# New place tables for a planned convolution and attention kernel, and another split of additions and products between VectorE and GpSimd

## The chip, the cores and the metric

The kernel runs on one core of a Trainium2 chip. Its time is the device time of one execution in microseconds (us). Five engines work beside each other, each through its own list of instructions in a fixed order: TensorE (PE; its weight loads are shown as PEld), VectorE (DVE), ScalarE (ACT), GpSimd (POOL) and SyncE (SP), which starts the DMAs. An instruction that waits holds up everything behind it on its engine.

## The reference

The input is x of shape 16 x 256 x 56 x 56 in float32. Two layers follow each other, each with a residual:

```python
x = x + _L0_conv_ref(_gn(x), ...)   # layer 0
x = x + _L1_conv_ref(_gn(x), ...)   # layer 1

# layer 0: sign of the input, then three dilated 3x3 convolutions (4 groups of
# 64 channels), each with binary weights, PReLU, shifts; summed; a norm over channels
for i, d in enumerate((1, 3, 5)):
    y = conv(sign(x + bias), bin_weight(w[i]), dilation=d, groups=4) + cb[i] - move1[i]
    y = where(y >= 0, y, alpha[i] * y) + move2[i]
    out = out + y
out = layer_norm_over_channels(out) * gamma + beta

# layer 1: 8 heads, 3x3 neighbourhood attention, 64 inner channels
q, k, v = qkv_w @ x + qkv_b
k = unfold(k) + dc_b + dwconv(k) + rpb       # 9 neighbours
v = unfold(v) + dc_b + dwconv(v)
attn = softmax((q * k).sum(channel), over the 9 neighbours)
out = proj_w @ (attn * v).sum(neighbours) + proj_b
```

`_gn` is a group norm with 32 groups.

## The kernel before

The 16 images are worked one after the other, each in two units (u = 0 and 1) of 128 partitions x 784 elements per channel group. An image goes through these stages, and each stage's operations are numbered from 0 in the order in which the program names them:

- `stats`, `norm0`, `sign`: ACT sums x and its squares (L570) and writes the signs (L594) into one set of tiles, `sgn`, that the convolutions of the image read.
- `conv0`, `conv1` (function `conv`): for each of 4 channel groups and 3 dilations, 36 matmuls on PE (L644), then ACT and DVE work on the PSUM banks (L663, L673, L678, L683). The third dilation's part is kept in a tile `rl` and added to `ct` at L689, an operation that goes through `either`.
- `var`, `root`, `mean`, `scale` (function `channel_norm`): the norm over channels; DVE subtracts the mean (L755) and scales (L765); the residual is added at L778, through `either`; ACT squares the sum (L782).
- `fold`: the second group norm is folded into the attention weights (L803 on POOL, L825 on PE). `qkv0`, `qkv1`: PE (L862), ACT writes q, k and v (L880).
- `prod0`, `prod1`: nine products of q with a shifted k for each unit (L915, through `either`). `term0`, `term1`: PE sums them over channels (L937).
- `soft0`, `soft1`: DVE transposes (L950, L972), maximum (L961), subtraction (L962), sum and reciprocal; ACT the exponential (L966); the product with the reciprocal goes through `either` (L971).
- `value0`, `value1` (function `attend`): for each neighbour PE spreads the weights (L986), DVE multiplies by v (L997), and a sum is kept in a tile `m`: the eight additions go through `either` (L1010); the tenth term is added by DVE (L1015).
- `proj0`, `proj1`: PE (L1027), and DVE adds the residual (L1037); then the store.

`either` emits an operation for GpSimd, or for VectorE where the operation's number stands in the table `ON_VECTOR` of its stage. A number of an operation that does not go through `either` has no effect; `soft0: (3,)` is of that kind, since operation 3 of `soft` is the subtraction that is always VectorE's.

No engine's order is written out. A class `Plan` collects all operations with what they read and write. Each has a place: `PERIOD` times its image's number, plus its entry in the table `ORDER`. A stage's name ends in `^` for the first image and in `$` for the last, and has no mark for the 14 images between. `Plan.emit` sorts by place and again and again takes the first operation whose inputs have been emitted and for which tiles are free; that gives every engine its order. A very low place therefore means "as soon as inputs and tiles allow". Tiles are few: four pairs of PSUM banks, five tiles `p`, three `m`, three `xt`, one set each of q, k and v.

Of the kernel before, what the change touches and what calls it, by code (L numbers as in the profile page):

```python
# [70 lines left out]
class Op:  # L71
    def __init__(self, place, emit, bufs):
# [6 lines left out]
PERIOD = 126.77  # L79
ORDER = {  # L80
    "first^": (-497.79,),
    "weights^": (
        -540.59, -276.27, -472.85, -121.02, 1.79, -121.01, -33.38, -40.08, -310.38, -8.87, -87.51, 10.76,
        -121.02, -347.57, 1.55, 12.14, -692.71, -322.65, -525.75, -97.97, -407.33, -195.77, -129.92,
        -262.19, -190.53, 10.75, -82.95, 37.61, -222.6, -117.13, -281.25, -133.31, 10.59, -72.96, 32.23,
        19.36, 12.13, -419.49, -79.69, -153.17, -260.86, -336.22,
    ),
    "second^": (
        61.97, 77.89, 59.61, -394.88, -231.37, -525.72, -317.93, 89.98, -351.54, -320.24, -170.43, -99.11,
    ),  # L90
    "start^": (
        -37.89, -330.85, 1.52, -87.54, -489.3, -643.61, -435.35, -192.82, -270.37, -108.68, -149.06,
        -278.79, -2012.74, -534.49, -502.69, -254.52, -75.19, 2.17, -46.62, -149.05, -203.19, -76.32,
        -254.55, -263.41, -527.85, -211.59, -216.21, -271.53, -72.59, -316.59, -388.45, -417.16, -608.13,
        -117.13, -276.59, 2.55, -250.76, -130.26, -368.41, -212.02, 3.89, -950.45, -407.55, -2282.23,
        -22.71, -513.74, -817.71, -764.21, -253.24, -287.46, -359.77, -118.23, -713.07, 35.52, 34.89,
        -41.66, -43.35, -258.45, -522.62, -624.21, -243.88, -289.86, -487.62, -51.52, -254.56, -583.14,
        -559.88, -516.73, -568.78, -425.01, -172.57, -282.11, -200.04,
    ),
    "conv0^": (  # L100
        -138.79, -276.48, -171.15, 36.21, -36.36, -506.31, -29.89, -243.93, 49.82, -784.24, -355.82,
        -293.64, -34.24, -130.27, -258.79, -37.09, 33.51, -139.51, -301.96, 37.42, 27.55, 69.97, 39.93,
        -631.57, -218.19, 72.59, 57.81, -355.85, -543.32, -414.61, 63.22, -365.99, 68.63, -658.09, 72.02,
        -37.08, -292.03, -552.29, -122.08, -314.82, -533.21, -570.33, -391.64, -204.63, -28.82, -120.38,
        -389.94, -254.56, -94.86, -138.42, -3.94, 38.26,
    ),
    "load0^": (65.19,),
    "var0^": (65.64, 75.51, -158.49, 8.33, -251.92, 76.54, -575.76, 19.98),
    "root0^": (-131.94, -804.87, -238.36, -98.85, -212.3, -189.81, -984.51, -512.94, -159.93, -30.98),
    "mean0^": (-97.24, -331.38, -195.77, 75.03, -395.09),  # L110
    "scale0^": (
        91.77, -641.16, -360.85, -13.99, -331.87, 86.31, -184.53, 116.95, -291.63, 40.3, -104.77, -87.96,
    ),
    "conv1^": (
        10.53, -123.25, -149.46, -256.19, 74.06, -430.73, 81.28, -172.15, 75.82, 79.15, -45.55, 40.04,
        104.27, -22.32, -430.47, -239.48, -70.69, 3.6, -363.54, 67.83, -366.01, -6.34, -357.82, -22.52,
        -363.55, -320.01, -24.08, -240.09, -79.2, -363.77, 72.55, -141.3, -472.94, -300.31, 71.95, -341.31,
        -597.68, -166.85, -717.64, 92.46, -1259.09, -15.64, -352.88, 110.8, -83.32, -291.95, -313.15, 99.61,
        -388.57, -291.93, 114.71, 117.83,
    ),  # L120
    "load1^": (102.36,),
    "var1^": (-386.62, 119.03, -291.96, -208.9, 118.89, 119.96, 118.87, -305.85),
    "root1^": (52.04, -107.23, -312.59, -252.65, 123.74, -365.58, -235.3, -252.39, 80.84, 129.09),
    "mean1^": (123.39, -252.34, -252.37, 174.57, 309.49),
    "scale1^": (
        -332.45, -19.11, 314.52, -290.35, 102.61, 53.91, -53.48, -75.89, 95.64, -376.56, -13.98, -564.86,
    ),
    "stats": (
        -520.49, -545.58, -642, -315.05, -176.75, -492.46, -200.46, -162.5, -509.22, -161.87, -990.44,
        -614.38,  # L130
    ),
    "norm0": (
        -161.34, -646.21, -938.09, -1057.59, -662.09, -384.09, -1551.11, -160.32, -1276.68, -1463.24,
        -832.05, -1040.34, -613.37,
    ),
    "sign": (
        -202.18, -586.86, -45.53, -270.83, -199.76, -289.25, -203.61, -361.03, -25.53, -52.28, 3.67,
        -140.17, -180.63,
    ),
    "fold^": (  # L140
        145.77, 141.33, -422.83, -178.85, -374.46, -84.54, 147.67, -137.8, 118.1, -608.09, -679.69, -447.31,
        145.34, -77.07, -209.83, -640.67, -14.43, 155.64, 108.99, 74.89, -585.9,
    ),
    "qkv0^": (159.28, -177.19, 155.62, -287.87, -250.25, 168.54, -126.25, 113.51),
    "qkv1^": (160.73, 41.41, 156.68, 70.72, -1211.22, 165.97, -243.93, 80.63),
    "prod0^": (150.82, 161.15, 24.4, -8.96, 31.22, -11.53, -53.88, 6.28, 141.75),
    "term0^": (155.72, -643.54, 161.18, 161.44, 164.94, 119.44, -38.49, -78.16, -27.17, -481.47),
    "soft0^": (-91.8, -221.41, 46.36, 171.67, -212.95, -177.41, -276.85, 174.63, -675.41),
    "value0^": (
        198.87, 87.32, -46.78, 99.31, 147.27, 12.38, 130.25, 202.92, 210.77, -882.03, 25.72, -45.62,  # L150
        -279.27, -209.89, 214.09, 11.82, -231.03, 118.43, -226.92, 120.47, 218.67, 35.37, 2.46, 219.08,
        54.55, 139.37, 224.04, 73.61,
    ),
    "proj0^": (241.44, -155.73, 238.72, -281.13, 237.12, -198.12, 241.45, -614.78, -21.47),
    "prod1^": (108.65, 170.6, -663.1, 146.13, 172.65, 130.53, 158.75, 116.81, 127.07),
    "term1^": (141.07, 3.93, 178.74, 170.95, 36.48, 146.64, -74.36, 187.17, 149.75, 35.59),
    "soft1^": (-168.11, 90, 199.36, 153.22, 211.29, 137.4, -148.25, 7.54, -91.76),
    "value1^": (
        234.98, -281, -60.34, -244.16, 14.04, 242.21, -649.29, -321.3, 241.48, -566.24, 29.38, 243.47,
        98.91, -12.5, 246.64, -315.58, 125.35, 248.65, -195.14, 252.25, 250.31, -123.38, 254.75, 196.65,  # L160
        243.91, 197.56, 254.85, 257.65,
    ),
    "proj1^": (220.75, 197.49, 266.19, 44.44, 147.62, 258.54, 286.77, -487.11, 26.44),
    "conv0": (
        -27.43, -142.44, -513.36, -534.67, -10.3, -679.71, -7.87, -218.09, -1.43, 1.81, -127.34, -17.42,
        -174.98, -181.46, -72.24, -170.42, -16.63, -10.21, -99.62, -7.59, -472.06, -7.47, -7.61, -245.96,
        -233.99, -1.12, -12.58, -10.43, -244.67, -82.72, -3.81, -376.9, -2.98, -17.39, 4.09, -38.29, -40.19,
        5.62, -55.73, -58.74, -426.88, -649.29, 12.56, -30.88, -515.52, -696.55, 16.57, -36.16, -650.3,
        -220.41, 14.98, -623.98,
    ),  # L170
    "load0": (-110.05,),
    "var0": (28.77, 33.56, -571.38, 34.22, 17.2, 34.4, -204.82, 34.42),
    "root0": (-142.24, -63.05, -111.28, 3.49, -236.77, -50.15, -553.8, 43.2, -262.19, -148.22),
    "mean0": (36.86, -115.55, -222.25, -138.25, -125.16),
    "scale0": (45.03, 55.24, -379.86, -482.52, 83.06, 94.44, -395.54, 65.7, 97.11, -254.89, 100, 76.09),
    "conv1": (
        16.45, -116.92, 17.5, 19.6, 34.21, -255.51, -457.16, -3.35, 52.2, 96.08, 97.34, -407.86, 102.86, 19,
        24.89, -189.61, -236.86, 28.25, -205.6, -61.71, -249.66, 26.4, -104.22, -1177.38, -72.59, -63.28,
        28.19, -22.53, -220.4, 5.96, 32.55, 28.21, -591.06, -242.18, 49.83, -522.83, -8.59, -273.01, 65.73,
        76.51, -456.7, -132.01, -483.95, 84.86, -276.27, 91.41, 72.9, 82.23, 90.98, -487.59, 72.91, -33.22,  # L180
    ),
    "load1": (39.53,),
    "var1": (112.96, 119.59, -102, 121.85, 121.97, 120.71, -8.64, -1308.77),
    "root1": (-365.25, -296.15, -555.28, -230.66, -772.77, -622.33, 123.71, -250.18, 109.37, 130.23),
    "mean1": (126.33, 109.37, 131.15, 134.74, 134.73),
    "scale1": (
        117.05, 130.9, -162.12, -135.91, -2.52, 9.73, -728.7, -385.62, 138.26, 52.19, -389.71, -755.04,
    ),
    "fold": (
        145.39, 144.6, -282.81, -292.97, -106.62, 39.92, 148.3, -270.26, -46.5, -103.11, -123.92, -462.47,  # L190
        119.25, 53.77, -321.01, -53.06, -355.43, 155.17, 80.85, 188.15, -608.21,
    ),
    "qkv0": (157.04, 45.26, 155.17, -324.99, -172.11, 164.97, -1481.52, -417.31),
# [1157 lines left out]
```

## Time and profile before

| what | value |
|---|---|
| time, median of 3 runs | 2100.16 us (2098.17 to 2104.22) |
| span of the profiled execution | 2099.5 us |
| profiled execution's own time against the median | its span is 0.7 us under the median; the page gives no other time for it |
| mean granted TensorE clock | 0.935 |
| PE busy | 1798.0 us, 86% |
| DVE busy | 1625.2 us, 77% |
| POOL busy | 1508.4 us, 72% |
| ACT busy | 1292.8 us, 62% |
| weights of the fold on POOL (L803): first of image 1, first of image 14 | 308.0 us, 1886.9 us |

The two starts of the last row are 13 images apart, so a middle image takes (1886.9 - 308.0) / 13 = 121.45 us. A busy share is an average over stages; what an engine holds up is seen in a stage's own row and in the chain of work that ended last.

### The profile page before, as it was taken

What the parts mean: (1) busy time and instruction counts of PE and PEld (TensorE: products, weight loads), DVE (VectorE), ACT (ScalarE), POOL (GpSimd) and SP (SyncE); (2) the same over time, 40 slices, a digit from 0 to 9 for tenths busy, and PEclk for the clock granted to TensorE, in tenths of its full rate; (3) what the DMA queues carried; (4) which work ended last, traced back from release to release, by engine and by line L of the source; (5) the groups of instructions that cost most, each with busy time, mean ns of one, the idle gap of its engine ahead of it and who ended that gap; (6) DMA issues with size and microseconds to landing.
All of it is one profiled execution on the core that took longest, in us unless ns stands there. A gap on an engine that the chain in (4) does not pass through costs nothing.

```text
span 2099.5 us, 71196 instructions
## 1 busy us (share of the span) xinstructions
PE 1798.0 (86%) x31770; PEld 906.3 (43%) x31770; DVE 1625.2 (77%) x2240; ACT 1292.8 (62%) x1733; POOL 1508.4 (72%) x884
## 2 busy tenths in 40 slices
PE   5667799898989989898989989898998989899694
PEld 4444254353535445353534435353443535344241
DVE  7565696968788696878879697877969687796876
ACT  6785575667667565767666576775757677463310
POOL 2233968878796887879597777968788786977714
PEclk8879999899999999999999999999999999999886
DMA  6760435535363654536364452637455353232212
GB/s 167 171 137 18 97 81 130 126 80 131 80 143 83 141 113 94 127 73 139 82 146 108 105 129 68 136 77 167 87 112 130 83 122 90 60 65 63 63 32 62
DMA packets 102420, 216.24 MB, mean 103 GB/s; under 512 B 10720, under 2 KB 84832, under 8 KB 102112
## 3 DMA queue, kind: packets, MB, share of 16 engines
q1 hardware_dynamic: 102112, 211.68, 45.0%
q8 instruction: 249, 4.08, 0.8%
q14 instruction: 59, 0.48, 0.1%
HBM read 154.85 MB, written 51.38 MB: 98 GB/s over the span
## 4 chain that ended last, share of the span: by engine, by line
PE 48%; DVE 27%; ACT 10%; issue 8%; POOL 4%; DMA 2%; SPq 0%; DVEq 0%; POOLq 0%; ACTq 0%
PE banks L644 16%; PE banks L862 12%; PE banks L937 7%; DVE m L997 5%; PE banks L986 4%; DVE xt L1037 4%; ACT xh L570 4%; PE banks L697 4%; DVE ct L765 3%; DVE ct L683 2%; ACT banks L678 2%; POOL m L1010 2%; DVE rl L683 2%; PE banks L1027 2%; DVE at L972 2%
## 5 line engine op out<-in xcount | busy, mean ns | idle before, releaser
L644 PE MATMUL banks<-sgn,wconv 64*64 64x392 bf16 x13824 | 674.3, 341 | 42.7 <-DVE rl L683 10.5
L1010 POOL TENSOR_TENSOR m<-m 128x784 f32<-128x784 f32 x252 | 469.7, 1864 | 169.1 <-DVE m L997 159.0
L644 PEld LDWEIGHTS <-wconv 64*64 64x64 bf16 x13824 | 441.5, 108 | 316.6 <-issue 144.4
L915 POOL TENSOR_TENSOR p<-qt,kt 128x784 f32<-128x784 f32 x273 | 473.1, 1768 | 108.8 <-PE banks L937 56.8
L678 ACT ACTIVATE banks<-banks,cbi,csc 128x784 f32<-128x784 f32 x384 | 373.0, 974 | 141.2 <-DVE ct L673 139.8
L689 POOL TENSOR_TENSOR ct<-ct,rl 128x784 f32<-128x784 f32 x128 | 237.9, 1859 | 247.0 <-DVE ct L683 99.9
L986 PE MATMUL banks<-at,wv 64*32 64x392 f32 x5120 | 315.6, 567 | 94.1 <-DVE m L997 49.9
L683 DVE SCALAR_TENSOR_TENSOR ct<-banks,oalpha,ct 128x784 f32<-128x784 f32 x256 | 262.0, 1028 | 84.9 <-ACT banks L678 82.7
L997 DVE TENSOR_TENSOR m<-banks,vt 128x784 f32<-128x784 f32 x288 | 274.6, 964 | 65.7 <-PE banks L986 59.3
L862 PE MATMUL banks<-xt,wf 64*64 64x392 f32 x3072 | 265.4, 495 | 3.9 <-DVE ct L755 3.9
L778 POOL TENSOR_TENSOR xt<-xt,ct 128x784 f32<-128x784 f32 x125 | 240.1, 1932 | 25.4 <-DVE ct L765 23.8
L937 PE MATMUL banks<-p,wk 32*64 32x392 f32 x4608 | 230.5, 499 | 11.7 <-POOL p L915 9.4
L673 DVE SCALAR_TENSOR_TENSOR ct<-banks,asc,ct 128x784 f32<-128x784 f32 x128 | 130.6, 1029 | 120.6 <-PE banks L644 117.1
L570 ACT ACTIVATE xh<-xh 128x1568 f32<-128x1568 f32 x120 | 180.9, 1508 | 7.2 <-DMA xh<-in_x 5.0
L986 PEld LDWEIGHTS banks<-at,wv 64*32 64x32 f32 x5120 | 67.3, 113 | 265.4 <-DVE m L997 106.1
L670 ACT ACTIVATE rl<-banks,asc 128x784 f32<-128x784 f32 x128 | 116.6, 911 | 103.6 <-POOL ct L689 59.1
L862 PEld LDWEIGHTS banks<-xt,wf 64*64 64x64 f32 x3072 | 114.3, 134 | 143.1 <-issue 131.0
L663 ACT ACTIVATE ct<-banks,mv,asc 128x784 f32<-128x784 f32 x128 | 128.3, 1003 | 49.1 <-PE banks L644 49.0
L683 DVE SCALAR_TENSOR_TENSOR rl<-banks,oalpha,rl 128x784 f32<-128x784 f32 x128 | 130.7, 1021 | 30.9 <-ACT banks L678 27.4
L1027 PE MATMUL banks<-m,wp 64*64 64x392 f32 x1024 | 116.2, 542 | 44.7 <-DVE xt L1037 24.7
L782 ACT ACTIVATE ct<-xt,pr 128x784 f32<-128x784 f32 x128 | 121.1, 947 | 42.0 <-POOL xt L778 34.3
L937 PEld LDWEIGHTS banks<-p,wk 32*64 32x64 f32 x4608 | 90.7, 131 | 118.4 <-issue 60.5
(111 smaller groups left out, 1961.8 us busy)
## 6 DMA issues: line engine op xcount, KB each, us to landing
xh<-in_x SPq DMA_DIRECT2D x248, 392.0 KB, 5.4
xt<-in_x SPq DMA_DIRECT2D x128, 392.0 KB, 7.0
out<-xt SPq DMA_DIRECT2D x128, 392.0 KB, 5.9
sgn<-sgn SPq DMA_DIRECT2D x128, 41.2 KB, 3.3
p<-in_w SPq DMA_DIRECT2D x12, 144.0 KB, 5.1
wq<-in_wqkv SPq DMA_DIRECT2D x1, 384.0 KB, 7.5
p<-in_wk_b SPq DMA_DIRECT2D x1, 320.0 KB, 6.9
p<-in_wk_c SPq DMA_DIRECT2D x1, 320.0 KB, 7.1
```

The source lines that it names most:

```text
L570: lambda func=func, col=col: nc.scalar.activation(inside(g) if b == 0 else image(xh), image(xh), func, accum_out=sums[:, col : col + 1]),
L644: nc.tensor.matmul(out=ps[q * GC : (q + 1) * GC, h, 0:SN], lhsT=wconv[h * GC : (h + 1) * GC, g, d, tap, :], rhs=sgn[g][h * GC : (h + 1) * ...
L678: lambda: nc.scalar.activation(n(), n(), AF.Relu, bias=cbi[:, g, s], scale=csc[:, g, s]),
L683: lambda: nc.vector.scalar_tensor_tensor(to.tile, n(), oalpha[:, g, s], to.tile, ALU.mult, ALU.add),
L689: lambda e: e.tensor_tensor(ct.tile, ct.tile, to.tile, ALU.add),
L778: lambda e, g=g: e.tensor_tensor(xt[:, g], xt[:, g], ct[g].tile, ALU.add),
L862: nc.tensor.matmul(out=ps[h * D : (h + 1) * D, q, 0:SN], lhsT=wf[q * GC : (q + 1) * GC, g, j, :], rhs=xt[q * GC : (q + 1) * GC, g, h, :], ...
L915: e.tensor_tensor(p.tile.rearrange("p x (r w) -> p x r w", w=W), _view(qt[:, 0, u * SN :], [(NU * SN + LANES, 2), (W, SR), (1, W)]), shift ...
L937: nc.tensor.matmul(out=ps[rt // 2][q * 64 : (q + 1) * 64, rt % 2, 0:n], lhsT=wk[r, j, :], rhs=rhs, start=s == 0, stop=s == 9,)
L986: nc.tensor.matmul(out=ps[rt * 32 : (rt + 1) * 32, q, 0:SN], lhsT=wv[q * 64 : (q + 1) * 64, j, :], rhs=at[q * 64 : (q + 1) * 64, rt, 0:SN] ...
L997: lambda j=j, m=m, ps=ps: nc.vector.tensor_tensor(m.tile.rearrange("p x (r w) -> p x r w", w=W), _view(ps[:, 0, :], [(512, 2), (W, SR), (1 ...
L1010: lambda e, m=m, acc=acc: e.tensor_tensor(acc.tile, acc.tile, m.tile, ALU.add),
```

## The change

Only tables differ. Every place is new, in units ten times smaller: `PERIOD` goes from 126.77 to 1233, and all entries of `ORDER` are whole numbers of that unit. `ON_VECTOR` is another. The program, the tiles and the arithmetic are the same, apart from which engine makes an addition or a product. A few stages of the middle images, and the whole of `ON_VECTOR`:

```diff
-PERIOD = 126.77
+PERIOD = 1233
 ORDER = {
...
-    "fold": (
-        145.39, 144.6, -282.81, -292.97, -106.62, 39.92, 148.3, -270.26, -46.5, -103.11, -123.92, -462.47,
-        119.25, 53.77, -321.01, -53.06, -355.43, 155.17, 80.85, 188.15, -608.21,
-    ),
+    "fold": (
+        1446, 683, -648, 321, 760, -4459, 424, 1459, 1254, -332, -110, 189, 188, 187, 186, -111, 1458, 1473,
+        556, 1228, 654,
+    ),
...
-    "prod0": (-19.47, -15.56, -19.52, -19.54, -9.65, -21.62, -60.46, -51.82, -46.06),
+    "prod0": (
+        658, -4846, -5150, 946, 601, 600, 1566, -5123, -4498,
+    ),
...
-    "soft0": (-41.86, -679.7, -542.92, 170.13, -417.32, 171.79, -33.82, 176.05, -128.14),
+    "soft0": (
+        1424, 798, -3067, -9321, 1632, -11063, -11031, 962, 1675,
+    ),
...
-    "value0": (
-        181.87, -930.05, 187.56, -630.23, 197.18, 210.12, -352.25, -424.15, 146.81, -310.05, 33.96, 216.06,
-        -870.49, 217.34, 67.04, -416.39, 61.68, -225.97, 199.7, 218.15, 219.99, 199.65, 224.72, 223.54,
-        -238.11, -183.76, 223.88, -281.12,
-    ),
+    "value0": (
+        1807, 1244, 1813, -9183, 1904, 1841, -1152, 1255, 1304, -9320, 2001, 1303, 1335, 1285, 1945, 1334,
+        1907, 2021, -9319, -1935, 2057, -6812, 2170, 1762, -9233, -181, 2066, -9269,
+    ),
...
-    "prod1": (-46.09, -46.11, -46.14, 54.21, 174.57, 9.36, 181.54, 181.52, 191.57),
+    "prod1": (
+        1614, -4783, -1232, -46, 810, 809, 1292, 1484, 1035,
+    ),
...
-    "proj1": (266.47, -198.81, 286.1, 20.21, 176.46, 258.74, 191.5, 262.9, -242.72),
+    "proj1": (
+        2509, 2579, 2476, 2569, 2618, 2210, 2620, 1142, 2177,
+    ),
...
 ON_VECTOR = {
-    "soft0^": (3,),
-    "soft1^": (3,),
-    "soft0": (3,),
-    "soft1": (3,),
-    "scale1$": (1, 4, 10),
+    "conv0$": (25, 38, 51),
+    "conv0^": (12, 38, 51),
+    "conv1$": (12, 51),
+    "conv1^": (25, 38),
+    "prod0": (0, 1, 3, 6),
     "prod0$": (0, 1, 2, 3, 4, 5, 6, 7, 8),
-    "soft0$": (3, 7),
-    "value0$": (10, 19, 25),
-    "prod1$": (0, 1, 2, 5, 6, 7),
-    "value1$": (25,),
+    "prod0^": (1, 3, 5, 7, 8),
+    "prod1": (6, 7),
+    "prod1$": (0, 1, 3),
+    "prod1^": (1, 2),
+    "scale0$": (7,),
+    "scale0^": (4, 7, 10),
+    "scale1$": (1,),
+    "scale1^": (1, 4),
+    "value0$": (19, 25),
+    "value0^": (4, 19),
+    "value1": (13,),
+    "value1$": (7, 13, 19, 22, 25),
 }
```

Operations that `either` emits for VectorE, over all 16 images:

| operation | before | after |
|---|---|---|
| product of q and k (L915) | 15 | 7 + 14 x 6 + 12 = 103 |
| addition of a value term (L1010) | 4 | 2 + 14 x 1 + 7 = 23 |
| addition of the third dilation (L689) | 0 | 5 + 5 = 10 |
| residual (L778) | 3 | 5 + 2 = 7 |
| softmax product (L971) | 1 | 0 |
| all | 23 | 143 |

## The prediction

> **What bounds the kernel now.** I read the page first. No engine is full over the whole span, and PE is the nearest to it.
>
> ```profile
> span 2099.5 us, 71196 instructions
> PE 1798.0 (86%) x31770; PEld 906.3 (43%) x31770; DVE 1625.2 (77%) x2240; ACT 1292.8 (62%) x1733; POOL 1508.4 (72%) x884
> PE 48%; DVE 27%; ACT 10%; issue 8%; POOL 4%; DMA 2%; SPq 0%; DVEq 0%; POOLq 0%; ACTq 0%
> ```
>
> The last of these lines is the chain of work that ended last, by engine. POOL, from which the change takes work, has 4% of it. DVE, which gets the work, has 27%.
>
> Then I cut the span into stretches: the head, one middle image (1018 to 1140 us), that image's attention in three parts, and the tail.
>
> ```profile
> core 0: us, PE busy (x) PEld busy (x) DVE busy (x) ACT busy (x) POOL busy (x), PEclk, DMA share, GB/s
> 0.00:166.00 166.00, 105.61 (x1878) 72.04 (x1882) 108.87 (x225) 126.99 (x164) 49.07 (x31) 0.84 0.65 150
> 1018.00:1140.00 122.00, 110.20 (x1997) 55.44 (x2000) 98.60 (x136) 81.05 (x109) 97.89 (x58) 0.96 0.50 113
> 1050.00:1067.00 17.00, 17.00 (x336) 8.01 (x328) 9.79 (x12) 5.99 (x10) 16.25 (x10) 1.00 0.45 101
> 1067.00:1092.00 25.00, 23.14 (x440) 10.88 (x432) 21.20 (x24) 15.21 (x18) 24.84 (x15) 1.00 0.84 181
> 1092.00:1112.00 20.00, 13.14 (x222) 5.29 (x222) 16.66 (x28) 17.42 (x26) 19.25 (x11) 0.83 0.59 145
> 2000.00:2100.00 100.00, 65.37 (x912) 24.94 (x912) 67.32 (x73) 8.44 (x12) 31.59 (x20) 0.79 0.22 49
> ```
>
> A middle image has PE busy for 110.2 of 122 us, so some 11 us can be won before PE is full. Of these 6.9 us lie in one stretch of 20 us (1092 to 1112), the value stage of unit 0, where PE's granted clock is down to 0.83 and POOL is busy for 19.25. In the product run before it (1050 to 1067) PE is full, POOL too, and DVE idles for 7.2 us.
>
> The waits of PE and its weight loads in the middle images (409 to 1870 us, 12 images) say for whom PE idles: mostly DVE.
>
> ```profile
> PE banks L986 <- DVE m L997: 36.5, 39, 1.8
> PE banks L986 <- DVE ct L683: 25.3, 13, 3.5
> PE banks L1027 <- DVE xt L1037: 23.0, 12, 1.9
> PE banks L514 <- ACT xh L570: 19.2, 6, 3.8
> ```
>
> Last, the groups with shapes kept apart give what an operation costs on each engine.
>
> ```profile
> L915 POOL TENSOR_TENSOR p<-qt,kt 128x784 f32<-128x784 f32 x273 | 473.1, 1768 | 108.8 <-PE banks L937 56.8 <-ACT qt L880 51.9 <-POOL p L915 0.2
> L1010 POOL TENSOR_TENSOR m<-m 128x784 f32<-128x784 f32 x252 | 469.7, 1864 | 169.1 <-DVE m L997 159.0 <-DVE m L1010 0.9
> L962 DVE TENSOR_TENSOR et<-et,mx 128x936 f32<-128x936 f32 x32 | 74.6, 2331 | 0.7
> L915 DVE TENSOR_TENSOR p<-qt,kt 128x784 f32<-128x784 f32 x15 | 13.5, 970 | 10.4 <-ACT qt L880 8.7 <-PE banks L937 1.7
> L971 DVE TENSOR_TENSOR et<-et,mx 128x936 f32<-128x936 f32 x1 | 1.1, 1134 | 0.0
> ```
>
> The two 936-element rows are the key. With POOL idle such an instruction takes 1.134 us on DVE; L962 takes 2.331 us on the mean, because POOL is at work beside it. In the image above it starts at 1070.97 us and takes 2.67, with a POOL product until about 1.67 us after its start; and the slowest of that run's POOL products takes 2.597 us where the median is 1.732. So two SBUF inputs on DVE and work on POOL exclude each other: each waits for the other's whole instruction.
>
> **The change part by part.** The sums are made against the profiled span, 2099.5 us; the median of the runs, 2100.16, is 0.7 us above it.
>
> *Moved operations.* 88 more products, 19 value additions, 10 additions of the third dilation and 4 residuals go to DVE, one softmax product goes back: 120 net. POOL loses 88 x 1.768 + 33 x 1.87 - 1.8 = 215.5 us of 1508. DVE gains at least 120 x 0.97 = 116 us (row L915 on DVE), and at most 120 x (0.97 + 1.20) = 260 us, with L962's mean wait of 2.331 - 1.134 = 1.20 us for each. DVE's busy time should end between 1740 and 1885 us. In a middle image seven operations move (products 0, 1, 3, 6 of unit 0; 6, 7 of unit 1; one value addition): POOL -12.5 us, DVE +6.8 to +15.2 on 98.6 of 122 us. I take 15.2, since L962 stands in the very run of POOL products that the moved ones come from. How much of it is seen? The four products of unit 0 (4 x 2.17 = 8.7 us) fall into the stretch where DVE idles for 7.2 us: 1.5 remain. The other three (6.5 us) fall into the softmax and value stretches, where DVE idles for only 3.8 us of 25 and 3.3 of 20, and I hide nothing. So 8 us, weighted with DVE's 27% of the chain, are 2.2 us an image, 14 x 2.2 = +31 us. Bounds: 0 (all in DVE's idle 23.4 us an image) and 14 x 15.2 x 0.27 = +57.
>
> Each moved product also brings its waits onto DVE: q from ACT (8.7 us once, in the row of L915 on DVE) and a free tile `p`, of which there are five. Behind a waiting product stand the conv evictions (L673, L683), and behind them PE's next banks. Bounds 0 and, with POOL's own waits of 108.8 us for 273 products, 0.4 us each: 0.4 x 84 x 0.27 = +9. I take 0, for a product placed late finds its inputs there; the 9 goes into the range.
>
> *POOL's relief.* 12.5 us an image at POOL's 4% of the chain: 14 x 0.5 = -7 us. Bounds: 0, since PE is full in the product run; and -14 x 6.9 = -97, if all of PE's idle time in the value stretch came from POOL's arriving there late.
>
> The SBUF — State Buffer page of the Trainium skill (section "SBUF: two separate sides") calls the port pair of VectorE and GpSimd an exclusive lock, held for a whole instruction, which speaks against this change. The 2.67 and 2.597 us above agree with it. By that rule POOL's relief would be an estimate of 12.5 - 6.8 = 5.7 us an image, so -3 us in place of -7. The GPSIMD Engine Reference (section 4.1, "Engine selection") has VectorE about twice as fast at elementwise work, and alone would leave out the 1.20 us of waiting: the sum of the moved operations would be 0 in place of +31.
>
> *Places.* The old places stand for times fairly well. I paired the order that the plan gives with each engine's instructions: from operation 9 of `conv0` (place 1.81) to 19 of `value0` (218.15) are 216.3 in the table and 210.7 us in the trace. But images follow each other by 126.77 in the table and by 121.45 us on the chip, a ratio of 0.958. In the same unit the new table has images 123.3 apart, and its latest places come earlier: `soft0` 167.5 for 176.05, `value0` 217.0 for 224.7, `proj1` 262.0 for 286.1, with `fold` where it was (operation 0 at 144.6 for 145.39). Taking the ratio over, an image takes 118.1 us, 3.3 less: 14 x 3.3 = -46 us. That is half of the value stretch's 6.9 us. The place is only a rank, so this is the weakest term: from below -14 x 7.6 = -107 us (to 113.8 us an image, DVE's 98.6 + 15.2), from above +14 x 3.4 = +48 (the ratio of the two periods the other way round, 121.45 x 1.028 = 124.9 us). I take the middle value because both old scales, 0.974 and 0.958, are near 1.
>
> *Head and tail.* In the head POOL is busy for 49 of 166 us, and 19 operations leave it over the first image: 0, with 10 us either way for the new order. In the tail a row of POOL additions of value terms lies on the chain (five of 1.87 us from 2068.96 us on); five of that unit's eight go to DVE, each 0.89 us shorter: -4.5; three products and a softmax product go back: 3 x 0.8 + 0.7 = +3.1. Together -1.
>
> *Sum:* -46 + 31 - 7 - 1 = -23; 2099.5 - 23 + 0.7 = 2077 us.
>
> **The rivals.**
>
> *DVE becomes the bound (slower).* If the seven operations find POOL holding the memory each time, and some lose two rounds (L962 took up to 5.183 us), DVE is busy for 114 us or more of an image and its waits for PE and ACT, 23.4 us now, no longer fit. Half of them, about 12 us, looks compressible; DVE's 98.6 + 15.2 + 12 = 125.8 us is then the image: 14 x 4.3 = +60, and a median near 2160; with part of the gain from places kept, 2115 to 2160. It decides from a wait of 12 / 7 - 0.97 = 0.7 us per moved operation on. For it: 1.20 us measured at L962. Against: with fewer POOL products there are fewer to collide with.
>
> *The new order stalls PE (slower).* PE's statistics matmul waits for ACT (L514 <- L570, 3.8 us at most in the middle images). One more such wait of 2 us an image makes +28: 2128.
>
> *Nothing moves (same).* PE is full where products run, and the value stretch is limited by the loop DVE m -> PE L986 anyway: 2100.
>
> *More is won.* PE's idle time goes down to DVE's floor: -107: about 1994, with half of it 2040.
>
> **How the numbers follow.** Forecast as summed 0.40 (2040 to 2093 us), more won 0.09, nothing 0.07, DVE as bound 0.30, stalls 0.14. Faster 0.49, same 0.07, slower 0.44; 0.3%, 6 us, is what a measurement tells from no change (the three runs lie 6 us apart). The range leaves out 0.09 below (under 2040) and about a quarter of the slower cases above 2155: 2040 to 2155. It has both signs; the likeliest case has 2040 to 2093 for itself.
>
> **What would show it.** Right: DVE busy 1740 to 1885 us, POOL near 1293 us plus up to 116 of blocked time; moved products on DVE with a mean near 2.2 us; images 118 to 120 us apart; PE busy over 15 of 20 us in the value stretch. Wrong: products on DVE near 1 us (no collision), or DVE above 110 us an image with PE's waits for DVE grown and images over 121.5 us apart; then DVE is the bound. Waits of PE for ACT grown: the order.

## The result, and the profile after

The changed kernel is slower: 2125.59 us (2121.56 to 2130.09) against 2101.15 us, a ratio of 1.0129 with a 95% interval of 1.0100 to 1.0157. The forecast had been 2077 us, faster. The profiled execution, the slowest of the four runs, has a span of 2127.6 us, 28.1 more than before.

From the page after: the span, the busy times, and the chain that ended last by engine.

```profile
span 2127.6 us, 71085 instructions
PE 1796.1 (84%) x31770; PEld 924.1 (43%) x31770; DVE 1812.1 (85%) x2360; ACT 1288.9 (61%) x1733; POOL 1365.5 (64%) x764
DVE 37%; PE 36%; ACT 9%; POOL 9%; issue 6%; DMA 2%; SPq 1%; DVEq 0%; POOLq 0%; ACTq 0%
```

DVE has taken the first place in the chain (27% before), and its busy time grew by 187 us; PE does the same work in a longer span. Line numbers after are those of before plus 86 (L915 is now L1001). In some of the experiments below they are up to 3 lower or 8 higher.

Where the 28.1 us came from is read off the starts of the fold (the order of the plan paired with each engine's instructions, as in the prediction). The start taken here and below is that of the fold's first operation on DVE, some 2.5 us ahead of its weights on POOL:

| stretch | before, us | after, us | difference |
|---|---|---|---|
| up to the fold of image 1 | 305.6 | 289.0 | -16.6 |
| 13 middle images (fold of image 1 to fold of image 14) | 13 x 121.45 | 13 x 124.81 | +43.7 |
| image 14 to image 15 | 113.9 | 117.0 | +3.1 |
| behind the last fold, to the end of the span | 101.2 | 99.1 | -2.1 |

So the loss is the middle images', 3.4 us each. One of them after the change, as a window (columns: stretch, length, busy time of each engine, granted clock, DMA share, GB/s):

```profile
1035.50:1160.10 124.60, 110.48 (x1989) 57.03 (x1984) 110.60 (x144) 80.99 (x109) 89.07 (x50) 0.96 0.48 108
```

PE has its 110 us as before; DVE went from 98.6 to 110.6, and POOL from 97.9 to 89.1. The groups with shapes kept apart show what became of the moved work:

```profile
L1001 POOL TENSOR_TENSOR p<-qt,kt 128x784 f32<-128x784 f32 x185 | 374.2, 2052 | 92.2 <-PE banks L1023 49.0 <-ACT kt L966 43.2
L1001 DVE TENSOR_TENSOR p<-qt,kt 128x784 f32<-128x784 f32 x103 | 177.4, 1766 | 12.7 <-ACT kt L966 11.6 <-PE banks L1023 1.1
L1096 DVE TENSOR_TENSOR m<-m 128x784 f32<-128x784 f32 x23 | 25.6, 1112 | 5.5 <-POOL m L1096 4.0
L1048 DVE TENSOR_TENSOR et<-et,mx 128x936 f32<-128x936 f32 x32 | 69.2, 2161 | 0.6
```

A product on DVE takes 1.766 us on the mean in place of 0.970, and those left on POOL take 2.052 in place of 1.768. The timeline of one middle image, first DVE and then POOL, shows the two engines taking turns:

```profile
1056.77 5.80 DVE L1001 TENSOR_TENSOR p<-qt,kt 128x784 f32<-128x784 f32 x3 [0.49 <-ACT kt L966]
1062.50 0.35 DVE L828 TENSOR_TENSOR lv<-banks,lv 128x196 f32<-128x196 f32 x1
...
1063.56 1.44 DVE L1001 TENSOR_TENSOR p<-qt,kt 128x784 f32<-128x784 f32 x1
1064.93 0.35 DVE L834 SCALAR_TENSOR_TENSOR lv<-banks,lv 128x196 f32<-128x196 f32 x1
1065.31 0.36 DVE L835 SCALAR_TENSOR_TENSOR lv<-lv,banks 128x196 f32<-128x196 f32 x1
1065.59 3.60 DVE L841 TENSOR_TENSOR ct<-ct,banks 128x784 f32<-128x784 f32 x4
1069.26 1.98 DVE L1036 STREAM_TRANSPOSE et<-banks 128x832 f32<-128x832 f32 x2
```

```profile
1056.82 14.76 POOL L1001 TENSOR_TENSOR p<-qt,kt 128x784 f32<-128x784 f32 x7 [2.48 <-ACT kt L966]
```

Three products on DVE last 5.80 us, where 2.7 would do; behind them stand the channel norm of the next image (L828 to L841) and the softmax (L1036). Means over the 14 middle images: products 1 and 3 of unit 0 take 2.37 and 2.40 us on DVE, 0 and 6 take 1.19 and 1.42, and those of POOL beside them (2, 4, 5, 7) 2.36 to 2.47.

The waits of PE in the middle images (414 to 1911 us, 12 images) have a new third row:

```profile
PE banks L1072 <- DVE ct L769: 37.3, 27, 1.8
PE banks L1113 <- DVE m L1101: 29.8, 12, 2.6
PE banks L1023 <- DVE ct L851: 29.4, 12, 3.7
PE banks L1072 <- DVE m L1083: 20.5, 31, 1.2
```

The first matmul of unit 1's terms (L1023) waits 2.45 us an image (29.4 / 12) for a PSUM bank that DVE frees only when it has scaled the channel norm (L851).

### The profile page after: what moved, and what is told of

Its sections match the earlier page's. It is cut to its first block, busy times and chain, and to the rows that moved or that the text cites. A ratio compares the mean times of both kernels' runs of the same rounds, so it can differ in the third digit from the quotient of the medians.

```text
span 2127.6 us, 71085 instructions
## 1 busy us (share of the span) xinstructions
PE 1796.1 (84%) x31770; PEld 924.1 (43%) x31770; DVE 1812.1 (85%) x2360; ACT 1288.9 (61%) x1733; POOL 1365.5 (64%) x764
## 4 chain that ended last, share of the span: by engine, by line
DVE 37%; PE 36%; ACT 9%; POOL 9%; issue 6%; DMA 2%; SPq 1%; DVEq 0%; POOLq 0%; ACTq 0%
PE banks L730 12%; PE banks L1023 8%; PE banks L948 6%; DVE m L1083 6%; PE banks L1072 5%; DVE ct L769 5%; ACT banks L764 4%; POOL m L1096 3%; DVE ct L851 3%; PE banks L783 3%; DVE p L1001 3%; DVE et L1048 3%; DVE xt L1123 3%; DVE ct L759 2%; DVE rl L769 2%
## 5 line engine op out<-in xcount | busy, mean ns | idle before, releaser
L730 PE MATMUL banks<-sgn,wconv 64*64 64x392 bf16 x13824 | 694.3, 348 | 48.4 <-DVE rl L769 17.7
L1096 POOL TENSOR_TENSOR m<-m 128x784 f32<-128x784 f32 x233 | 445.4, 1912 | 236.0 <-DVE m L1083 229.8
L730 PEld LDWEIGHTS <-wconv 64*64 64x64 bf16 x13824 | 450.5, 110 | 312.6 <-issue 140.0
L775 POOL TENSOR_TENSOR ct<-ct,rl 128x784 f32<-128x784 f32 x118 | 219.4, 1859 | 370.4 <-DVE ct L769 180.9
L1001 POOL TENSOR_TENSOR p<-qt,kt 128x784 f32<-128x784 f32 x185 | 374.2, 2052 | 92.2 <-PE banks L1023 49.0
L1072 PE MATMUL banks<-at,wv 64*32 64x392 f32 x5120 | 290.0, 531 | 93.6 <-DVE ct L769 41.4
L1023 PE MATMUL banks<-p,wk 32*64 32x392 f32 x4608 | 244.5, 519 | 25.5 <-DVE p L1001 12.9
L1001 DVE TENSOR_TENSOR p<-qt,kt 128x784 f32<-128x784 f32 x103 | 177.4, 1766 | 12.7 <-ACT kt L966 11.6
L749 ACT ACTIVATE ct<-banks,mv,asc 128x784 f32<-128x784 f32 x128 | 128.4, 1003 | 98.2 <-PE banks L730 97.9
L1023 PEld LDWEIGHTS banks<-p,wk 32*64 32x64 f32 x4608 | 98.7, 136 | 147.6 <-issue 39.9
L680 ACT ACTIVATE sgn<-xh,g 128x1568 bf16<-128x1568 f32 x64 | 105.4, 1647 | 69.0 <-PE banks L730 65.3
```

Of the source, the lines that this page charges most:

```text
L730: nc.tensor.matmul(out=ps[q * GC : (q + 1) * GC, h, 0:SN], lhsT=wconv[h * GC : (h + 1) * GC, g, d, tap, :], rhs=sgn[g][h * GC : (h + 1) * ...
L775: lambda e: e.tensor_tensor(ct.tile, ct.tile, to.tile, ALU.add),
L1001: e.tensor_tensor(p.tile.rearrange("p x (r w) -> p x r w", w=W), _view(qt[:, 0, u * SN :], [(NU * SN + LANES, 2), (W, SR), (1, W)]), shift ...
L1023: nc.tensor.matmul(out=ps[rt // 2][q * 64 : (q + 1) * 64, rt % 2, 0:n], lhsT=wk[r, j, :], rhs=rhs, start=s == 0, stop=s == 9,)
L1072: nc.tensor.matmul(out=ps[rt * 32 : (rt + 1) * 32, q, 0:SN], lhsT=wv[q * 64 : (q + 1) * 64, j, :], rhs=at[q * 64 : (q + 1) * 64, rt, 0:SN] ...
L1096: lambda e, m=m, acc=acc: e.tensor_tensor(acc.tile, acc.tile, m.tile, ALU.add),
```

## The experiments

The table gathers all of them. The ratio is to the kernel before, timed on the same chip beside each. Softmax start is the median start of unit 0's first transpose after the image's fold, over images 2 to 13; image length is the mean over 13 middle images; both come from one profile each. The profiled run lies within 9 us of its kernel's median, but for e3, where it is 19 us above; e3's image is by that up to 1.4 us too long in the table. Times of kernels that were measured on different chips are compared by their ratios.

| kernel | time, us | ratio (95% interval) | image, us | softmax start, us |
|---|---|---|---|---|
| before | 2101 | 1 | 121.45 | 33.0 |
| changed | 2125.6 | 1.0129 (1.0100 to 1.0157) | 124.81 | 33.8 |
| e1_places | 2247.6 | 1.0657 (1.0613 to 1.0700) | 129.80 | 37.5 |
| e2_choice | 2246.0 | 1.0672 (1.0643 to 1.0701) | 130.88 | 39.0 |
| e3_mid_back | 2195.9 | 1.0436 (1.0400 to 1.0472) | 131.14 | 37.5 |
| e4_one_input | 2096.2 | 0.9958 (0.9944 to 0.9972) | 122.67 | 32.3 |
| e5_unit0 | 2116.4 | 1.0089 (1.0059 to 1.0120) | 123.91 | 33.8 |
| e6_unit1 | 2205.2 | 1.0515 (1.0490 to 1.0541) | 130.02 | 37.5 |
| e7_on_act | 2106.1 | 1.0016 (0.9994 to 1.0037) | 123.34 | 32.8 |
| e8_k_first | 2195.3 | 1.0464 (1.0419 to 1.0508) | 129.24 | 38.4 |
| v1_unit0_all | 2145.0 | 1.0185 (1.0146 to 1.0224) | 126.59 | 34.5 |
| v2_unit0_only | 2149.1 | 1.0208 (1.0174 to 1.0243) | 126.51 | 34.5 |
| v3_one_input_unit0 | 2091.8 | 0.9940 (0.9920 to 0.9961) | 122.66 | 32.3 |
| w1_conv_later | 2105.2 | 0.9999 (0.9982 to 1.0017) | 122.79 | 33.8 |
| w2_conv_later_one_input | 2074.9 | 0.9854 (0.9828 to 0.9881) | 120.84 | 32.3 |
| w3_proj_later | 2110.1 | 1.0053 (1.0033 to 1.0074) | 123.34 | 33.8 |
| w4_value_add | 2108.6 | 1.0053 (1.0036 to 1.0070) | 123.19 | 33.8 |
| m1_first_new | 2163.7 | 1.0321 (1.0298 to 1.0345) | 120.26 | 33.1 |
| m2_ends_new | 2220.1 | 1.0603 (1.0578 to 1.0627) | 121.87 | 33.1 |
| m3_first_places | 2162.4 | 1.0320 (1.0295 to 1.0345) | 121.05 | 32.8 |

### Places and choice taken apart

The first two cross the tables. e1 has all places of the changed kernel and the old choice:

```diff
 ON_VECTOR = {
-    ... the new table
+    ... the old table
 }
```

> The new places with the old choice for VectorE. Theory A (the moved operations of the middle images, at 1.2 to 2.4 us each on VectorE, lengthen an image): an image falls from 124.8 back to about 121.5 us or less, while the head keeps its 16.6 us: about 2085 us. Theory B (the new order by itself is slower in the middle images, whoever makes the products): an image stays near 124.8 us and the time near 2125 us.

Measured: 2247.6 us, images of 129.80 us. e2 is the other corner, the old places with the new `ON_VECTOR`:

> The old places with the new choice for VectorE. Theory A: an image grows by about 3 us from 121.5, and the time goes to about 2130 to 2150 us, with nothing won in the head. Theory B: an image stays at 121.5 us and the time within 10 us of the kernel before, 2100.

Measured: 2246.0 us, images of 130.88 us. Neither theory stands. Each half of the change alone costs some 140 us, both together 25: the effects do not add up, and the prediction's way of summing them was wrong. e3 keeps the changed kernel and returns the moved operations of the middle images alone:

```diff
-    "prod0": (0, 1, 3, 6),
-    "prod1": (6, 7),
-    "value1": (13,),
```

> The changed kernel with the seven moved operations of each middle image back on GpSimd; the first and the last image keep the new choice. Theory A: an image near 121.5 us, and 14 x 3.3 = 46 us less than the changed kernel: about 2080 us. Theory B: within 10 us of the changed kernel, 2126.

Measured: 2195.9 us, 3.0% or some 65 us above the changed kernel by the ratios. In the new order the moves win that much. The trace shows where, in what PE does behind the fold's matmul (L825 before, L911 after). Before:

```profile
1039.65 1.57 PE L825 MATMUL banks<-wf,sq 128*128 128x192 f32 x8
1041.15 8.13 PE L862 MATMUL banks<-xt,wf 64*64 64x392 f32 x96
```

After:

```profile
1043.63 1.57 PE L911 MATMUL banks<-wf,sq 128*128 128x192 f32 x8
1045.36 1.75 PE L730 MATMUL banks<-sgn,wconv 64*64 64x392 bf16 x36 [0.16 <-DVE ct L769]
1047.12 2.86 PE L948 MATMUL banks<-xt,wf 64*64 64x392 f32 x32
...
1051.37 1.74 PE L730 MATMUL banks<-sgn,wconv 64*64 64x392 bf16 x36
1052.95 5.43 PE L948 MATMUL banks<-xt,wf 64*64 64x392 f32 x64
```

In the old order PE makes k for both units right behind the fold's matmul, and unit 0's products run from 16.1 to 31.7 us after the fold, all on POOL. In the new order two convolution groups (L730) and, in the lines left out, two groups of variance matmuls come before the second k, and the products start only at 21.3 us. POOL alone then ends them at 36.4 (e3); with four on DVE it is 32.7. The moved products pay for a later start.

What goes with the harm in the old order is seen in e2's timeline (image 7), DVE and then POOL:

```profile
1122.16 5.80 DVE L923 TENSOR_TENSOR p<-qt,kt 128x784 f32<-128x784 f32 x3 [4.72 <-ACT qt L888]
1127.89 1.02 DVE L681 SCALAR_TENSOR_TENSOR ct<-banks,asc,ct 128x784 f32<-128x784 f32 x1
```

```profile
1122.21 4.92 POOL L923 TENSOR_TENSOR p<-qt,kt 128x784 f32<-128x784 f32 x2 [3.62 <-ACT qt L888]
1136.82 1.74 POOL L923 TENSOR_TENSOR p<-qt,kt 128x784 f32<-128x784 f32 x1 [9.70 <-PE banks L945]
```

DVE waits 4.72 us for q with the products at the head of its queue, then takes 5.80 us for them, and the convolution's eviction (L681, L673 of before) comes 5.5 us later after the fold than in the same image before (21.9 against 16.4 us). ACT writes unit 1's q at 23.8 us after the fold in place of 19.7; the first term matmul reads the q of both units; the five tiles `p` stay full, and POOL stands still for 9.70 us. No run takes these steps apart in the old order, so this chain is read from the trace and not shown by an experiment.

### Which moves, and is it VectorE's load or the collision?

e4 keeps six instructions of 784 elements on VectorE, but with one SBUF input:

```diff
+                if e is nc.vector and 0 < b < NB - 1:
+                    e.tensor_reduce(
+                        p.tile.rearrange("p x (r w) -> p x r w", w=W),
+                        shifted(kt, u, j).unsqueeze(4), AX.X, ALU.add)
+                    return
                 e.tensor_tensor(
```

> The changed kernel, with each of the six moved products of a middle image replaced on VectorE by a reduction of the shifted k alone, over a length of one: one SBUF input in place of two, the same 784 elements, the factor q left out. It takes the collision with GpSimd away and keeps the instruction on VectorE. If the collision is what costs (six products of 11.1 us in place of 5.8, and GpSimd's products of 2.4 in place of 1.75): images 2 to 3 us shorter, about 2085 to 2100 us. If VectorE's time itself is what costs: at most 1 us an image, 2110 to 2126 us. Under theory B: no change, 2126 us.

Measured: 2096.2 us, 1.7% below the changed kernel by the ratios, and 0.4% faster than the kernel before. The groups of e4 (the stand-in, the products left on POOL):

```profile
L1002 DVE TENSOR_REDUCE p<-kt 128x784 f32<-128x784 f32 x84 | 77.4, 962 | 15.1 <-PE banks L1031 9.1 <-ACT kt L966 5.9
L1009 POOL TENSOR_TENSOR p<-qt,kt 128x784 f32<-128x784 f32 x185 | 335.3, 1842 | 108.9 <-PE banks L1031 65.8 <-ACT kt L966 43.1
```

On the same engine an instruction of the same size takes 0.962 us beside a working POOL when it reads SBUF once; with two inputs the six take 1.86 on the mean (the means 1.19, 2.37, 2.40, 1.42, 1.85, 1.91 over 6). The kind of instruction is not what decides: in the changed kernel the two largest groups of DVE's other tensor_tensor instructions of 784 elements, which read SBUF once and PSUM once, never took more than 0.975 us (shortest, median and longest, in ns):

```profile
L1083 DVE TENSOR_TENSOR m<-banks,vt x288: 912/965/975, 219.6 to 2106.6; 128x784 f32<-128x784 f32 x144
L841 DVE TENSOR_TENSOR ct<-ct,banks x128: 955/961/970, 106.4 to 2013.4; 128x784 f32<-128x784 f32 x128
```

Nor is it the wait for q, which the stand-in need not have: unit 0's q is written at 13.4 us after the fold in the changed kernel, and unit 0's products start at 21.3 us in both. The collision goes with the second SBUF input. e5 and e6 split the moves of the middle images by unit:

```diff
 e5:
-    "prod1": (6, 7),
-    "value1": (13,),
 e6:
-    "prod0": (0, 1, 3, 6),
```

> The changed kernel with unit 1's two products and the value addition of each middle image back on GpSimd; unit 0's four products stay on VectorE. Theory C (the new order starts the products later after the fold, 21.3 us against 16.1, and the moved products make up for it by shortening the run): unit 0's four matter most, so an image stays near the changed kernel's 124.8 us or grows by up to 2 us: 2115 to 2155 us. Theory D (VectorE's load is the bound): three operations less on VectorE, about 5 us, make an image 1 to 3 us shorter: 2085 to 2110 us.

> The changed kernel with unit 0's four products of each middle image back on GpSimd; unit 1's two and the value addition stay on VectorE. Theory C: the product run of unit 0 is 15 us again and starts late, so an image grows by 3 to 5 us: 2165 to 2195 us. Theory D: shorter images, 2085 to 2110 us.

Measured: 2116.4 and 2205.2 us. Unit 0's four products carry all that the moves win; unit 1's three operations win nothing, and rather cost some 0.4% beside unit 0's (the intervals of e5 and of the changed kernel overlap) and 0.8% without them (e6 against e3, where the intervals do not overlap). e7 makes the six moved products on ScalarE:

```diff
+                if e is nc.vector and 0 < b < NB - 1:
+                    nc.scalar.copy(
+                        p.tile.rearrange("p x (r w) -> p x r w", w=W), shifted(kt, u, j))
+                    return
                 e.tensor_tensor(
```

> The changed kernel with the six moved products of a middle image replaced by copies of the shifted k on ScalarE (the factor q is left out), so that neither VectorE nor GpSimd has them. Against the run with one SBUF input on VectorE (2096 us, images of 122.7 us) it takes VectorE's 5.8 us an image away. Theory D: 2 to 4 us an image shorter, 2040 to 2070 us. Theory C: VectorE's time is hidden, so about 2090 to 2100 us, or longer where ScalarE's own queue delays the copies.

Measured: 2106.1 us, ratio 1.0016, against e4's 0.9958. Taking 5.8 us an image of load from VectorE (1664.3 us busy in place of e4's 1731.3) wins nothing. e7 alone would not settle it, since ScalarE's queue now has the copies, at a cost of its own that is not known. But e3 and e6 say the same: VectorE is busy for 1677.7 and 1731.9 us there, in place of the changed kernel's 1812.1, and an image is 5 to 6 us longer. So VectorE's sum of work is not the bound. v3 repeats e4 for unit 0's four products alone, on top of e5:

> Unit 0's four products of a middle image as reductions with one SBUF input on VectorE (the factor q is left out), unit 1's operations on GpSimd. It differs from the run with unit 0's four true products alone (2116 us) only in the collisions of unit 0. If unit 0's collisions make most of the 30 us: 2090 to 2100 us; if unit 1's do: 2110 us or more.

Measured: 2091.8 us, 1.5% below e5 by the ratios (some 31 us). Taking all six collisions away was worth 1.7% (e4), so unit 0's are nearly the whole price of colliding; an image falls from 123.91 to 122.66 us in the profiles.

### An earlier start, and all nine products on VectorE

If the late start is what the moves have to make up for, an earlier one should win. e8 gives PE k for both units first:

```diff
     "qkv0": (
-        1472, -6055, 1539, -6029, 1041, 1613, -12592, -6503,
+        1472, -6055, 1475, -6029, 1041, 1613, -12592, -6503,
     "qkv1": (
-        1546, 416, 1500, 930, 916, 1652, -2564, -2566,
+        1546, 416, 1474, 930, 916, 1652, -2564, -2566,
```

> The changed kernel with two places altered in the middle images, so that PE makes k for both units right after the fold's matmul and before a convolution and the variance matmuls that the new order has between them; the choice for VectorE stays. Theory C: products start about 4 to 5 us earlier after the fold, and an image is 1 to 4 us shorter: 2070 to 2112 us. Theory D: the load of VectorE is the same, so within 10 us of the changed kernel: 2116 to 2136 us.

Measured: 2195.3 us, 70 more. The expectation failed although the products do start at 16.4 us. DVE and then POOL in e8:

```profile
1086.96 5.81 DVE L1001 TENSOR_TENSOR p<-qt,kt 128x784 f32<-128x784 f32 x3 [4.00 <-ACT kt L966]
1092.69 1.02 DVE L759 SCALAR_TENSOR_TENSOR ct<-banks,asc,ct 128x784 f32<-128x784 f32 x1
```

```profile
1087.01 4.92 POOL L1001 TENSOR_TENSOR p<-qt,kt 128x784 f32<-128x784 f32 x2 [11.98 <-ACT kt L966]
1102.08 1.73 POOL L1001 TENSOR_TENSOR p<-qt,kt 128x784 f32<-128x784 f32 x1 [4.29 <-PE banks L1023]
```

It is e2's picture again: DVE waits 4.00 us at the products and takes 5.81 for them, with the convolution's evictions (L759) behind; unit 1's q is written at 27.1 us after the fold in place of 23.0, and unit 0's product run ends at 37.3. It looks as if the late k of the new order lets DVE clear the evictions first; this, too, is read from the trace alone.

v1 removes the collisions of unit 0 with the true products, by giving all nine to VectorE; v2 also returns unit 1's operations:

```diff
-    "prod0": (0, 1, 3, 6),
+    "prod0": (0, 1, 2, 3, 4, 5, 6, 7, 8),
```

> The changed kernel, with all nine products of unit 0 of a middle image on VectorE in place of four; the result is complete. In the changed kernel VectorE spends 7.4 us on four of them because of the collisions; nine without collisions, as in the last image at 0.885 us from start to start, are 8.0 us. Collision theory: the run of unit 0 ends near 30 us after the fold in place of 32.7, VectorE's busy time grows by less than 1 us an image, and the time is 2070 to 2110 us. Load theory (VectorE as the bound, collisions only shift work): VectorE's five more products cost 3 us or more an image: 2165 us or more.

> As the run before, with unit 1's two products and the value addition of a middle image back on GpSimd. Collision theory: 2060 to 2105 us, up to 10 us less than the run before, as with four products (2116 against 2126). Load theory: 2150 us or more.

Measured: 2145.0 and 2149.1 us. v1 misses both theories; v2 ends 1 us under the load theory's 2150, but not by load: its VectorE is busy for 1745.7 us, e5's for 1736.9, and v2 is 1.2% slower than e5. In v1 VectorE's busy time is that of the changed kernel (1806.9 us against 1812.1), and unit 0's run does end earlier, at 30.4 us. But VectorE's timeline has the rest of its queue behind it:

```profile
1065.68 4.52 DVE L1001 TENSOR_TENSOR p<-qt,kt 128x784 f32<-128x784 f32 x5 [0.49 <-ACT kt L966]
...
1071.18 3.62 DVE L1001 TENSOR_TENSOR p<-qt,kt 128x784 f32<-128x784 f32 x4
...
1075.39 3.61 DVE L841 TENSOR_TENSOR ct<-ct,banks 128x784 f32<-128x784 f32 x4
1078.91 1.97 DVE L1036 STREAM_TRANSPOSE et<-banks 128x832 f32<-128x832 f32 x2
```

From the first product to the softmax's transpose it takes 13.23 us (1065.68 to 1078.91), where the changed kernel takes 12.49 (1056.77 to 1069.26). So the softmax starts at 34.5 us after the fold, 0.7 later, and the image is 1.8 us longer in the profiles (the times differ by 0.6%, and their intervals overlap). In the table, the kernels with the new places unaltered have longer images the later the softmax starts, about 1.5 us an image per us (122.7 at 32.3; 123.9 and 124.8 at 33.8; 126.6 at 34.5; 130 to 131 at 37.5); e8, with two places altered, lies 2 to 3 us below that line. That fits VectorE's order, not its sum of work, as what sets the image. The slope is above one in part because the term matmuls themselves take longer there (235.0 us in e4, 260.8 to 266.7 in e1, e3 and e6, some 2 us an image); the rest of it is not shown.

### The rest of the new order

Without collisions in unit 0 (v3, e4) an image is still 1.2 us longer than before. w1 and w2 test the new wait for the bank: they place one convolution group behind unit 1's first terms, on top of e5 and of v3.

```diff
     "conv1": (
-        ... 164, -7309, -577, 443, -3801, ...
+        ... 164, -7309, -577, 459, -3801, ...
```

> Unit 0's four true products on VectorE (2116 us), and in the middle images one convolution group (operation 34 of conv1) placed behind unit 1's first term matmuls in place of ahead of them. If PE's new wait for the bank (L1023 for L851, 29.4 us in 12 images) is what makes the rest: the wait shrinks by half or more, and an image is 1 to 2 us shorter: 2088 to 2104 us. If another wait takes its place: 2110 us or more.

> The same with unit 0's products as reductions with one SBUF input (2092 us; the factor q is left out). If the bank's wait makes the rest: images of 121.5 us or less, 2065 to 2080 us. If another wait takes its place: 2088 us or more.

Measured: 2105.2 us (ratio 0.9999) and 2074.9 us (0.9854). The former is 0.9% below e5, the latter 0.9% below v3 (some 19 us each), and their images are 1.1 and 1.8 us shorter in the profiles. In w1 the first term matmul no longer waits for the scaling, and what is left of the 29.4 us is the convolution's wait (L728):

```profile
PE banks L728 <- DVE ct L849: 15.7, 13, 2.5
```

w1 ends 1 us above the range expected for it (2088 to 2104), w2 inside its own. Measured beside each other on one chip, the two differ by 30.3 us in collisions alone. w3 and w4 go on from w1. w3 treats the second wait of PE, for the last value addition, in the same way, and w4 also returns `value1`'s addition to VectorE:

```diff
     "proj1": (
-        2509, 2579, 2476, 2569, 2618, 2210, 2620, 1142, 2177,
+        2509, 2579, 2504, 2569, 2618, 2210, 2620, 1142, 2177,
 w4 besides:
+    "value1": (13,),
```

> The 2105 us version (unit 0's four true products on VectorE, the convolution behind unit 1's first terms), with the first projection matmul of unit 1 in each middle image placed behind one more convolution group. If the wait for the last addition is paid in full: 1 to 1.7 us an image less, 2082 to 2092 us. If the addition's delay only shows at the next operation: 2100 us or more.

> As the run before, and the one value addition of unit 1 back on VectorE, as in the changed kernel, where it took 0.98 us each time without a collision. If only collisions make moved operations dear: the same as the run before or up to 10 us less. If VectorE's load counts: up to 10 us more.

Measured: 2110.1 and 2108.6 us, both 1.0053. The row in w3's waits of PE tells why:

```profile
PE banks L728 <- DVE m L1099: 29.1, 11, 2.6
```

The same 2.6 us is now waited for by the convolution (L728): what is missing is the bank that the addition frees, whoever asks for it first. The value addition, which meets no POOL work on the way (0.98 us), costs nothing either way. No version with the true products beat the kernel before; w1 is level with it.

### The head alone

Three kernels ask whether the 16.6 us of the head can be had by itself: the tables of the first image (`^`) new, all else old (m1); the last image (`$`) too (m2); the first image's places without its moves (m3).

```diff
 PERIOD = 126.77
 ORDER = {
     ... stages with ^ (m2: and with $) from the new table, divided by 10; the others old
 ON_VECTOR = {
     ... stages with ^ (m2: and with $; m3: neither) from the new table; the others old
```

> The kernel before with the places and the choice of the first image from the changed kernel (in the old unit), all else old. If the head's gain of the changed kernel (the fold of the second image 16.6 us earlier) lies in the first image's own places and moves and not in what follows: middle images near 121.5 us, and 2085 us (2080 to 2092). If it comes from the shorter distance between images: 2100 us or more.

> As the run before, and the last image too with the new places and choice. The changed kernel is 2.1 us shorter behind the last fold, so if the tail carries over: 2 us below the run with the first image alone, 2083 us; if the last image's new places need the middle's new ones: 5 to 30 us above it.

> The first image with its new places but with the old choice (none of its 19 operations on VectorE), all else old. If the gain of the head is the places': near the run with both, 2085 us. If places and moves belong together there as in the middle images: a loss, 2105 us or more.

Measured: 2163.7, 2220.1 and 2162.4 us. The middle images stay at 120 to 122 us, but the fold of image 1 comes at 376.3 us (m1) in place of 305.6, and in m2 the last interval grows to 162.4 us from 113.9. Images overlap, so an image's places fit only its neighbours'. m1 and m3 differ by nothing: the moves of the first image are not what counts at this seam. Within the new order they do count. e1 and e3 differ only in the choice for the first and the last image, and the fold of image 1 starts at 315.9 us in e1 and at 290.7 in e3; with the new choice in the old order (e2) it starts at 320.4. So in the head, too, the new places alone (e1) and the new choice alone (e2) each lose 10 to 15 us against the 305.6 of before, and both together win 16.6 (one profile each).

## Why the prediction was wrong

**What bounds the kernel:** right. DVE's share of the chain was the right place to fear (27% before, 37% after), and PE got a new wait for DVE.

**Moved operations, +31 us:** the size was right by luck, since the way to it was not. DVE's busy time (1812 us, forecast 1740 to 1885) and POOL's (1365.5, forecast 1293 and up to 116 of blocked time) came out as worked out; a moved product in a middle image takes 1.86 us, where I took 2.17. Taking unit 0's collisions away is worth 30.3 us (w1 against w2), 31 (e5 against v3). But I had counted unit 0's four products as nearly hidden in DVE's idle time and charged unit 1's three; it is the other way round, since unit 0's stand ahead of the norm and the softmax on DVE's queue. The hidden time was idle time of the old order.

**POOL's relief, -7 us:** mis-sized by a factor of about ten, in the new order. There the moves win some 65 us net of their collisions (e3), and some 100 us where they do not collide (e3 against e4, 4.8% by the ratios). The run of products starts 5.2 us later than before, and POOL alone ends it 3.7 us later than with DVE's help (36.4 against 32.7 us). In the old order the moves lose (e2).

**Places, -46 us: the step that failed.** I took a shorter `PERIOD` and earlier places for a shorter image. The new places with the old choice have images of 129.80 us, with the new one 124.81, and without collisions 122.7: 1.2 us longer than before, so +17 us over 14 images in place of -46. Of what the order costs, PE's new wait for one bank (L1023 for L851) is 1.1 to 1.8 us an image, by what its removal is worth (w1, w2); with it and unit 0's collisions gone the time is 2074.9 us, 0.6 us an image under the kernel before, still far from 3.3. A place is a rank in a sort: the same table, 123.3 apart, gave images of 124.81 or 129.80 us on the chip by the choice that went with it.

**Head and tail:** the tail's -1 measured -2.1. One of its five additions was on VectorE before already, so that four move, and its sum should have been about 0. For the head I took 0 and it was -16.6, outside the 10 us allowed for the order; the other runs with the changed first image have the fold of image 1 at 284 to 298 us against 305.6, so the sign holds.

**The rivals:** the first had the right place (the collision) and, with images of up to 125.8 us, nearly the right length, but named the wrong cause: VectorE's load as the bound. That 2125.6 us lies in its 2115 to 2160 is therefore luck. e7 takes 5.8 us an image of load away and wins nothing over e4, and e3 and e6 have less load and longer images. The sign that the prediction gave for it (DVE above 110 us an image, images over 121.5 us, PE's waits for DVE grown) came true, with 110.6 and 124.81 us, but it does not tell DVE's load from DVE's order. The second, a new stall of PE, was true as well, but for a bank held by DVE and not for ACT. Half of the fourth's -107 us ends at 2047 us and not at 2040. The slower cases had 0.44 together, and the likeliest part of the range still lay below.

**The pages weighed:** the exclusive lock that the SBUF — State Buffer page ("SBUF: two separate sides") describes is what e4 shows, 0.962 us with one input and 1.86 with two. That VectorE is about twice as fast at such work, as the GPSIMD Engine Reference (section 4.1) has it, holds where POOL is idle (0.970 against 1.768 us) and not beside it. The 0 that the prediction names for that page does not follow its own rule of hiding nothing of three operations: 3 x 0.97 x 0.27 x 14 are +11.

## What to carry to other kernels

A move between two engines that exclude each other on SBUF paid here only where it shortened a run that something waits for; count its price where it stands in the receiving engine's queue, by what is behind it, and not by that engine's idle share. An order and an assignment that were made for each other cannot be costed one by one: here each alone lost 140 us and both together 25. And a wait for a PSUM bank goes with the bank: putting another operation in front paid once here (w1), and once only changed who waits (w3).

## What was not expected of the hardware

The prediction had the collision itself: a VectorE instruction with two SBUF inputs waited for POOL's instruction (2.4 us in place of 0.97), and POOL's next for VectorE's (2.4 in place of 1.7). What it did not have is where it ends: a VectorE reduction of the same 784 elements with one SBUF input ran beside the same POOL work at 0.962 us. And even with the two engines taking turns, unit 0's nine products took 11.4 us in place of 15.1 on POOL alone in the same order (e3), and v1's on VectorE alone, without a collision, 9.1.
